# A selective scan with an FFT filter: Latin-square units, with the first group's du*B made by TensorE and ScalarE

## The chip, the cores and the metric

The kernel runs on one core of one Trainium2 chip. The metric is the device time of one execution in microseconds (us); the lower, the better. Engines are named as in the profile: PE is TensorE (PEld its weight loads), DVE is VectorE, ACT is ScalarE, POOL is GpSimd, SP is SyncE, which issues nearly all DMAs here.

## The reference, cut to what matters

The first layer is a Mamba block over 4 images of 128 channels and 128x128 pixels, taken as sequences of 16384 steps. Only the part around the scan matters for the change:

```python
u = silu(causal_conv4(x_in) + conv_b)                  # 256 channels d
dt, B, C = split(u @ x_proj_w.T, [8, 16, 16])          # 16 states s
delta = softplus(dt @ dt_proj_w.T + dt_proj_b)
A = -exp(A_log)                                        # [256, 16]
def step(h, (d, B, C, u)):
    h = h * exp(d[:, None] * A) + d[:, None] * B[None, :] * u[:, None]
    return h, einsum('ds,s->d', h, C)
y = (scan(step) + u * D) * silu(z)
out = y @ out_proj_w.T
x1 = silu(group_norm(out)) + x
```

The second layer group-normalizes x1, takes a small softmax of pooled features ("aggregation"), filters x1 through a 2D FFT with weights from that softmax, and adds half of x1. The change does not touch the second layer's FFT part.

## The kernel before, in words

`block0` computes the Mamba block and the statistics for the second layer; `block1` computes the FFT part, after it.

**Tiling.** A sequence is cut into chunks of T = 512 steps: 32 chunks per image, 128 in all. In a chunk there are 256 x 16 = 4096 independent scans. They are laid on partitions as 32 channels x 4 states (partition = 4 x channel + state), so a chunk has 32 tiles of 128 x 512: two halves of the channels (j = 0, 1), four groups of states (g = 0 to 3, the field SQ = 4 states wide), and four blocks of 32 channels (m, or ND). A **unit** is the four tiles of one (j, g); a **pair** is two tiles of it. A chunk has 8 units and NP = 16 pairs.

**Work of one pair** (`exps`, L308, and `scans`, L321 to L325): ACT computes da = exp(delta * A) from delta, repeated over the four states, into a PSUM tile of two banks; DVE runs two scans h = da * h + hb; the product of h with C goes back into hb, on DVE (L324, then h overwrites da in PSUM) or on POOL (L324, then h is in SBUF, since `dve` is false); ACT copies the last column (L325, "last") as the start of the next chunk. **Work of one unit**: POOL computes hb = du * B for all four tiles at once (`dbu`, L293); PE sums h * C over the states with a 0/1 matrix (`sums`, L337), into one PSUM bank for each half j, which `sums` opens with u * D (L334).

**Who does the products with C.** Seven of a chunk's 16 pairs go to POOL: the first pair of each unit but one; the other nine stay on DVE.

**What makes a chunk** (`pre`): load of x, three matmul stages (h1, xm, z), the convolution as 8 matmuls (L221, each two records in the trace), silu (L226, L227), the projections xd and dt, softplus (L261), du = delta * u on POOL (L269). Partitions are rearranged through DRAM: delta and du are written out and read back repeated over the four states (`rep_load`, L277), B and C are written out and read back repeated over the 32 channels (`bc_load`, L246). `post` gates y with silu(z) (L349), multiplies by the output matrix (L354), copies (L361), stores and takes statistics (L365).

**Normalization and aggregation** (`finish`): for the image before, two tiles at a time in each of 16 chunks are normalized (`norm_load`, `norm_act` L432, `norm_mm` L437, `norm_dve` L441 and L442), and two tiles in each of the next 16 chunks aggregated (`agg_load` L461, `agg_mm` L465, `agg_act` L469). For the last image there is no scan beside it.

**The order.** It is written out by hand: every piece of work has a slot and a phase, and within one slot the phases follow in a fixed order. Slots count pairs, so slot n holds the scans of pair n. Each engine runs its instructions in the order in which they are issued. The exps of a pair are issued one slot ahead, du*B two slots ahead of the unit, the sums two slots behind the unit's last pair.

```python
        for n in range(n_chunks * NP):
            todo[n - 1, "exps"].append(partial(exps, n))
            todo[n, "scans"].append(partial(scans, n))
            if n % 2 == 0:
                todo[n - 2, "dbu"].append(partial(dbu, n // 2))
            else:
                todo[n + 2, "sums"].append(partial(sums, n // 2))
        ...
                for phase in ("sums", "pe", "exps", "act", "pool", "dbu", "scans", "dve", "end"):
```

In the lists that `pre` and `post` return, slot numbers are relative to the start of the chunk before: number 16 is the first slot of the chunk itself. The text numbers slots of a chunk from 0 to 15; the preparation of the next chunk stands in the same slots (its number 2 is slot 2, its number -6 slot 10).

**PSUM.** Eight banks: two for `psum()` (all matmul stages), two for y (one for each half), four for da (two tiles of two banks).

## Time and profile before

| | |
|---|---|
| median of 8 runs | 8235.5 us (8233.16 to 8238.89) |
| the profiled execution's own time | 8235.23 us |
| its span, first to last instruction | 8233.4 us |
| block 0 with scans running | to about 7162 us |
| normalization and aggregation of the last image | 7162 to about 7358 us |
| block 1 | about 7358 us to the end |
| busy: DVE, POOL, PE, ACT | 7666.5, 7521.4, 6049.0, 5262.8 us |
| granted PE clock | 0.846 on average |

How to read the lines that follow. A group of the page reads: line, engine, operation, names (out <- in), shapes, count, then the total busy time in us, the mean of one in ns, and the idle time of the engine just ahead of these instructions with what ended it. A line of the timeline reads: start in us, length in us, engine, line, operation, names, shape, and how many consecutive instructions were merged; in brackets the wait ahead of it and what ended that. A line of the windows reads: from:to, length, busy time and count of PE, PEld, DVE, ACT and POOL, then the granted PE clock, the share of the DMA engines and GB/s.

### The profile page before, as it was taken

The page shows a single profiled execution, that of the slowest core. Times are in us where ns is not written, and L with a number is a line of the kernel's source. Part 1 is how long each engine was busy: PE and PEld are TensorE (multiplying, and loading weights), DVE is VectorE, ACT ScalarE, POOL GpSimd, SP SyncE. Part 2 cuts the span into 40 slices and gives each one's busy share as a digit, 9 for nine tenths or more (in the row PEclk, how much of TensorE's full clock was granted, in tenths as well). Part 3 has the DMA queues.
Part 4 walks back from the last instruction along what each step waited for, and adds up shares of the span by engine and source line. Part 5 has one row for each costly group of instructions (what it writes and reads, how often), then busy time and mean ns, then how long its engine had stood idle before and what let it go on. Part 6 is the DMA issues. An engine that isn't in the chain of part 4 may idle for free.

```text
span 8233.4 us, 73103 instructions
## 1 busy us (share of the span) xinstructions
PE 6049.0 (73%) x20532; PEld 2223.2 (27%) x20532; DVE 7666.5 (93%) x6640; ACT 5262.8 (64%) x9495; POOL 7521.4 (91%) x2500
## 2 busy tenths in 40 slices
PE   6776676777777777777777777777776777569999
PEld 1121121111111122221111222221111222138888
DVE  6999999999999999999999999999999999839999
ACT  5666666666666676666666666666666767534444
POOL 7999999999999999999999999999999999716665
PEclk8777778778888887888889888888998888779999
DMA  4444444444454444444454444445454444454443
GB/s 151 137 144 155 145 147 137 151 147 162 167 172 153 168 161 155 147 166 166 159 175 161 158 160 159 153 156 175 155 176 163 150 159 157 142 170 115 117 123 95
DMA packets 838679, 1257.45 MB, mean 153 GB/s; under 512 B 78200, under 2 KB 276864, under 8 KB 838272
## 3 DMA queue, kind: packets, MB, share of 16 engines
q1 hardware_dynamic: 835760, 1252.43, 46.1%
q8 instruction: 162, 2.65, 0.1%
q14 instruction: 245, 2.01, 0.1%
q10 hardware_dynamic: 2512, 0.36, 0.0%
HBM read 1009.22 MB, written 243.27 MB: 152 GB/s over the span
## 4 chain that ended last, share of the span: by engine, by line
DVE 35%; issue 25%; POOL 20%; ACT 14%; DMA 2%; PE 2%; SPq 1%; DVEq 0%; POOLq 0%; ACTq 0%
DVE da L321 14%; POOL hb L293 11%; DVE h L321 8%; POOL hb L324 7%; ACT da L308 5%; DVE hb L324 3%; DVE wb L590 3%; POOL du L269 2%; ACT L308 2%; ACT L226 2%; ACT u L226 2%; ACT zs L227 1%; DVE im L617 1%; DVE ii L620 1%; DVE ot L644 1%
## 5 line engine op out<-in xcount | busy, mean ns | idle before, releaser
L293 POOL TENSOR_TENSOR hb<-rdu,rB 128x2048 f32<-128x2048 f32 x1024 | 4631.8, 4523 | 17.9 <-DMA rdu<-dd 17.9
L321 DVE TENSOR_TENSOR_SCAN da<-da,st,hb 128x512 f32<-128x512 f32 x2232 | 2862.5, 1282 | 42.0 <-ACT da L308 2.5
L308 ACT ACTIVATE da<-rdelta,amat 128x512 f32<-128x512 f32 x4096 | 2831.9, 691 | 102.8 <-ACT st L325 0.2
L337 PE MATMUL y<-hb,sel 128*32 128x512 f32 x8192 | 1660.5, 741 | 1314.7 <-POOL hb L324 1147.1
L321 DVE TENSOR_TENSOR_SCAN h<-da,st,hb 128x512 f32<-128x512 f32 x1736 | 2127.8, 1267 | 221.5 <-ACT st L325 109.7
L324 POOL TENSOR_TENSOR hb<-h,rC 128x1024 f32<-128x1024 f32 x896 | 2103.3, 2347 | 102.9 <-DVE h L321 100.6
L324 DVE TENSOR_TENSOR hb<-da,rC 128x1024 f32<-128x1024 f32 x1152 | 1410.3, 1224 | 51.9
L325 ACT COPY st<-da 128x2 f32<-128x2 f32 x1152 | 184.4, 160 | 1929.6 <-DVE hb L324 1928.9
L221 PE MATMUL pp_cv<-xm,wck 128*128 128x512 f32 x2048 | 975.1, 631 | 57.0 <-ACT zs L215 57.0
L337 PEld LDWEIGHTS y<-hb,sel 128*32 128x32 f32 x8192 | 218.8, 116 | 2550.9 <-POOL hb L324 1780.3
L221 PEld LDWEIGHTS pp_cv<-xm,wck 128*128 128x128 f32 x2048 | 402.4, 202 | 658.3 <-issue 450.4
L616 POOL TENSOR_TENSOR re<-sq 128x520 f32<-128x520 f32 x64 | 84.8, 1325 | 464.4 <-ACT sq L614 464.3
L186 PE MATMUL pp_h<-xt,w 128*128 128x512 f32 x512 | 349.8, 807 | 199.1 <-DVE of L441 80.7
L354 PE MATMUL pp_o<-yg,wo 128*128 128x512 f32 x512 | 379.1, 881 | 126.1 <-ACT u L226 126.0
L210 PE MATMUL pp_z<-xm,win 128*128 128x512 f32 x512 | 359.8, 840 | 72.6 <-ACT xm L204 72.6
L269 POOL TENSOR_TENSOR du<-delta,u 128x512 f32<-128x512 f32 x256 | 319.3, 1267 | 60.8 <-ACT delta L261 60.8
L253 PE MATMUL pp_dt<-xd,wdt 8*128 8x512 f32 x512 | 300.4, 712 | 77.6 <-ACT xd L238 77.6
L196 PE MATMUL pp_xm<-h,w 128*128 128x512 f32 x512 | 296.3, 707 | 60.0 <-ACT h L191 60.0
L308 ACT ACT_TABLE_LOAD x261 | 334.9, 1283 | 3.0
L325 ACT COPY st<-h 128x2 f32<-128x2 f32 x896 | 171.6, 192 | 247.1 <-DVE h L321 236.4
L437 PE MATMUL pp_xr<-xr,ident 128*128 128x512 f32 x256 | 206.0, 948 | 160.3 <-DMA xr<-in_x 69.1
L590 DVE SCALAR_TENSOR_TENSOR wb<-ft,wts,wb 128x1040 f32<-128x1040 f32 x192 | 296.8, 1547 | 4.4
(107 smaller groups left out, 7372.8 us busy)
## 6 DMA issues: line engine op xcount, KB each, us to landing
rdelta<-dd SPq DMA_DIRECT2D x1024, 256.0 KB, 3.5
rdu<-dd SPq DMA_DIRECT2D x1024, 256.0 KB, 4.7
rB<-bc SPq DMA_DIRECT2D x512, 256.0 KB, 3.7
rC<-bc SPq DMA_DIRECT2D x512, 256.0 KB, 5.1
dd<-delta SPq DMA_DIRECT2D x256, 256.0 KB, 5.0
dd<-du SPq DMA_DIRECT2D x256, 256.0 KB, 3.3
ft<-in_filt_w SPq DMA_DIRECT2D x64, 520.0 KB, 7.1
xt<-in_x SPq DMA_DIRECT2D x128, 256.0 KB, 5.2
```

Source lines behind the costliest of these rows:

```text
L186: nc.tensor.matmul(ps["h", j], s.w1[:, j * P : (j + 1) * P], d["xt"], start=True, stop=True)
L210: nc.tensor.matmul(ps["z", j], w, d["xm"][:, HALO:], start=True, stop=True)
L221: nc.tensor.matmul(ps["cv", j], w, d["xm"][:, t : t + T], start=t == 0, stop=t == KC - 1)
L269: nc.gpsimd.tensor_tensor(du, d["dn"][:, j, :], d["u"][:, j, :], ALU.mult)
L293: nc.gpsimd.tensor_tensor(hb, d["du", j], d["B"][:, g : g + 1, :].to_broadcast([P, ND, T]), ALU.mult)
L308: nc.scalar.activation(da[:, q, :], d["delta", j][:, m + q, :], AF.Exp, scale=s.amat[:, c : c + 1])
L321: nc.vector.tensor_tensor_scan(h[:, q, :], da[:, q, :], hb[:, m + q, :], init, ALU.mult, ALU.add)
L324: eng.tensor_tensor(hb[:, m : m + 2, :], h, cr, ALU.mult)
L325: nc.scalar.copy(last, h[:, :, T - 1])
L337: nc.tensor.matmul(y[q * DG : (q + 1) * DG, :], s.sel, d["hb", j, g][:, q, :], start=False, stop=g == NG - 1)
L354: nc.tensor.matmul(d["po"], s.wo[:, j, :], d["yg"][:, j, :], start=j == 0, stop=j == NH - 1)
L590: nc.vector.scalar_tensor_tensor(wb, ft[:, f], s.wts[b][0:H, f : f + 1], wb, ALU.mult, ALU.add)
```

## The change

**Latin square.** A unit is no longer one group of states with four channel blocks. Unit r of a half takes position p = 0 to 3, where position p is always group p, and its channel block is `place(r, p) = (p - r) % 4`. So each unit holds one tile of every group, the four units of a half cover all (group, block) pairs, and position 0 of every unit is a tile of group 0.

**du*B of group 0** is not computed on POOL any more. In the preparation of the chunk, PE transposes du and the projections xd (time goes onto partitions), ACT multiplies the transposed du by B of each of the four states, a number per partition there, and writes the results interleaved, so that channel and state stand in the order of the scan tiles (`bt`). For every unit, PE transposes four 128x128 pieces of `bt` into a PSUM bank `b0` (`dbu_turn`), which the first scan of the unit reads directly. `dbu` on POOL covers positions 1 to 3; where `place` wraps round it needs two instructions. B of group 0 is not read back from DRAM any more.

**Pairs.** The first pair of every unit has its product with C on POOL (8 a chunk); in odd chunks one second pair too (j = 1, r = 2). DVE keeps 8, or 7 in odd chunks.

**PSUM.** y has one bank for both halves; one bank is for the transposes of the preparation, one for `b0`. The da tile of odd slots has one buffer of two banks; for even slots da is split into two tiles, the first in SBUF (two buffers), the second in PSUM (one).

**SBUF.** h1 and delta share one tag, delta has a name of its own beside the repeated delta, du stays in a buffer of its own (as before) and is now read by PE too. The gates write in place into zs. xt has one buffer (two before); the normalization's tiles have two (xr) and share three with o (four each before). The convolution's taps are loaded into a pool that is closed again, on SP.

**Order.** There are two new phases, "turn" at the head and "gate" ahead of "scans". "gate" holds the normalization's adds (`norm_dve`), which stood behind the scans; the gates of y stay in "dve", behind the scans. Both du products are issued in slot 7.

The diff, cut to its core:

```diff
-        psd = pool("psd", 2, space=PSUM)
+        pst = pool("pst", 1, space=PSUM)
+        psd = pool("psd", 1, space=PSUM)
...
-                xt = d["xt"] = p2.tile([P, T], F32, tag="xt", name=f"xt_{k}")
+                xt = d["xt"] = p1.tile([P, T], F32, tag="xt", name=f"xt_{k}")
...
-                d["h1"] = p1.tile([P, NH, T], F32, tag="h1", name=f"h1_{k}")
+                d["h1"] = p1.tile([P, NH, T], F32, tag="hd", name=f"h1_{k}")
...
-                    t = d[tag] = p2.tile([P, NG, T], F32, tag=f"r{tag}", name=f"r{tag}_{k}")
-                    for g in range(NG):
+                    t = d[tag] = p2.tile([P, NG - 1 + q, T], F32, tag=f"r{tag}", name=f"r{tag}_{k}")
+                    for g in range(1 - q, NG):
...
+            def xd_turn():
+                ps["xt"] = turned(f"xdt_{k}")
+                for t in range(NT):
+                    nc.tensor.transpose(ps["xt"][:, t, 0:NX], d["xd"][:, t * P : (t + 1) * P], s.ident[0:NX, 0:NX])
+
+            def xd_turn_act():
+                d["xdt"] = p1.tile([P, NT, NX], F32, tag="xdt", name=f"xdt_{k}")
+                nc.scalar.copy(d["xdt"], ps["xt"][:, :, 0:NX])
+
+            def du_turn(h):
+                ps["dut"] = turned(f"dut_{k}_{h}")
+                for t in range(2):
+                    for j in range(NH):
+                        at = (2 * h + t) * P
+                        nc.tensor.transpose(
+                            ps["dut"][:, 2 * t + j, :], d["du"][:, j, at : at + P], s.ident
+                        )
+
+            def bt_act(h, n0, n1):
+                if h == n0 == 0:
+                    d["bt"] = p2.tile([P, NT, NH * ND, DG, SQ], F32, tag="bt", name=f"bt_{k}")
+                for n in range(n0, n1):
+                    t, q = divmod(n, SQ)
+                    src = ps["dut"][:, 2 * t : 2 * t + 2, :].rearrange("p j (g d) -> p (j g) d", d=DG)
+                    nc.scalar.activation(
+                        d["bt"][:, 2 * h + t, :, :, q], src, AF.Copy, scale=d["xdt"][:, 2 * h + t, R + q : R + q + 1]
+                    )
...
-                (2, "act", silu_act), (3, "pe", xd_mm), (4, "act", xd_act), (5, "pe", dt_mm), (5, "act", bc_load),
-                (6, "act", dt_act), (7, "pool", partial(du_pool, 0)), (8, "pool", partial(du_pool, 1)),
-                (9, "act", partial(rep_load, 0)), (16, "pe", partial(rep_load, 1)),
+                (2, "act", silu_act), (3, "pe", xd_mm), (4, "act", xd_act), (5, "pe", dt_mm), (5, "pe", xd_turn),
+                (5, "act", bc_load), (6, "act", dt_act), (7, "act", xd_turn_act), (7, "pool", partial(du_pool, 0)),
+                (7, "pool", partial(du_pool, 1)), (9, "pe", partial(du_turn, 0)), (9, "act", partial(rep_load, 0)),
+                (10, "act", partial(bt_act, 0, 0, 3)), (11, "act", partial(bt_act, 0, 3, 8)),
+                (12, "turn", partial(du_turn, 1)), (12, "act", partial(bt_act, 1, 0, 2)),
+                (13, "act", partial(bt_act, 1, 2, 6)), (14, "act", partial(bt_act, 1, 6, 8)),
+                (16, "pe", partial(rep_load, 1)),
...
+        def place(r, p):
+            return (p - r) % ND
...
-            hb = d["hb", j, g] = p4.tile([P, ND, T], F32, tag="hb", name=f"hb_{k}_{j}_{g}")
-            nc.gpsimd.tensor_tensor(hb, d["du", j], d["B"][:, g : g + 1, :].to_broadcast([P, ND, T]), ALU.mult)
+            hb = d["hb", j, r] = hpool.tile([P, ND, T], F32, tag="hb", name=f"hb_{k}_{j}_{r}")
+            p = 1
+            while p < NG:
+                m = place(r, p)
+                n = min(NG - p, ND - m)
+                nc.gpsimd.tensor_tensor(
+                    hb[:, p : p + n, :], d["du", j][:, m : m + n, :], d["B"][:, p - 1 : p - 1 + n, :], ALU.mult
+                )
+                p += n
...
+        def dbu_turn(n):
+            k, j, r, p = pair(n)
+            d = st[k]
+            if p == 0:
+                b = d["b0"] = psd.tile([P, T], F32, tag="b0", name=f"b0_{k}_{j}_{r}")
+                for t in range(NT):
+                    src = d["bt"][:, t, j * ND + place(r, 0), :, :].rearrange("p d s -> p (d s)")
+                    nc.tensor.transpose(b[:, t * P : (t + 1) * P], src, s.ident)
...
-            da = d["da", j, g, m] = psd.tile([P, 2, T], F32, tag="da", name=f"da_{k}_{j}_{g}_{m}")
+            if p:
+                da = psd.tile([P, 2, T], F32, tag="da", name=f"da_{k}_{j}_{r}_{p}")
+                d["da", p] = [da[:, 0, :], da[:, 1, :]]
+                d["h", j, r] = da
+            else:
+                d["da", p] = [
+                    p2.tile([P, T], F32, tag="da", name=f"da0_{k}_{j}_{r}"),
+                    psd.tile([P, T], F32, tag="da1", name=f"da1_{k}_{j}_{r}"),
+                ]
...
-            dve = m > 0 or (j == 0 and g == NG - 1)
+            dve = p > 0 and not (k % 2 and j == 1 and r == 2)
...
+                b = hb[:, q, :] if p + q else d.pop("b0")
...
-                y = d["y", j] = psy.tile([P, T], F32, tag=f"y{j}", name=f"y_{k}_{j}")
+                y = d["y", j] = psy.tile([P, T], F32, tag="y", name=f"y_{k}_{j}")
...
-                nc.vector.tensor_mul(d["yg"][:, j, :], d["zs"][:, j, :], d["y", j])
+                nc.vector.tensor_mul(d["zs"][:, j, :], d["zs"][:, j, :], d["y", j])
...
-                xr = g["x", i] = p4.tile([P, T], F32, tag="xr", name=f"xr_{b}_{i}")
-                o = g["o", i] = p4.tile([P, T], F32, tag="of", name=f"of_{b}_{i}")
+                xr = g["x", i] = p2.tile([P, T], F32, tag="xr", name=f"xr_{b}_{i}")
+                o = g["o", i] = p2.tile([P, T], F32, tag="o", name=f"of_{b}_{i}", bufs=3)
...
-                x1 = g["x1", i] = p4.tile([P, T], F32, tag="xr", name=f"x1_{b}_{i}")
+                x1 = g["x1", i] = p2.tile([P, T], F32, tag="xr", name=f"x1_{b}_{i}")
...
-                    (c + 7, "pe", partial(norm_mm, i)), (c + 8, "dve", partial(norm_dve, i)),
+                    (c + 7, "pe", partial(norm_mm, i)), (c + 8, "gate", partial(norm_dve, i)),
...
+            todo[n - 1, "turn"].append(partial(dbu_turn, n))
...
-                for phase in ("sums", "pe", "exps", "act", "pool", "dbu", "scans", "dve", "end"):
+                for phase in ("turn", "sums", "pe", "exps", "act", "pool", "dbu", "gate", "scans", "dve", "end"):
```

## The prediction

> **What bounds the kernel now.** I read the page's first part, then its costliest groups, then the windows and the timeline inside one chunk, and last the two tails of block 0.
>
> ```profile
> PE 6049.0 (73%) x20532; PEld 2223.2 (27%) x20532; DVE 7666.5 (93%) x6640; ACT 5262.8 (64%) x9495; POOL 7521.4 (91%) x2500
> L293 POOL TENSOR_TENSOR hb<-rdu,rB 128x2048 f32<-128x2048 f32 x1024 | 4631.8, 4523 | 17.9 <-DMA rdu<-dd 17.9
> L324 POOL TENSOR_TENSOR hb<-h,rC 128x1024 f32<-128x1024 f32 x896 | 2103.3, 2347 | 102.9 <-DVE h L321 100.6
> L324 DVE TENSOR_TENSOR hb<-da,rC 128x1024 f32<-128x1024 f32 x1152 | 1410.3, 1224 | 51.9
> ```
>
> Two engines are full, VectorE and GpSimd; ScalarE has a third of its time free. GpSimd's largest group is the product du*B, of which the change takes a quarter away. Which of the two ends a chunk differs by stage:
>
> ```profile
> 2300.00:2357.20 57.20, 41.92 (x116) 11.56 (x112) 54.31 (x49) 37.70 (x68) 54.60 (x18) 0.85 0.49 167
> 3000.00:3054.50 54.50, 36.81 (x111) 9.96 (x109) 52.05 (x45) 37.72 (x70) 54.50 (x18) 0.82 0.46 156
> L227 ACT ACTIVATE zs<-zs x128: 1046/1055/1059, 31.4 to 7065.7; 128x1024 f32<-128x1024 f32 x128
> ```
>
> The columns are span, then PE, weight loads, DVE, ACT, POOL, clock, DMA. L227 runs once a chunk, so its starts mark the period. In a plain chunk (3000) it is 54.5 us and POOL is busy for all of it; in a chunk with normalization (2300) it is 57.2 and POOL has gaps. From 31.4 to 7065.7 are 127 periods, 7034.3 us; with periods of 54.5 and 57.2 that is about 85 of the first and 42 of the second.
>
> Inside a chunk, what one instruction really takes is the distance to the next start:
>
> ```profile
> 2299.26 2.45 DVE L321 TENSOR_TENSOR_SCAN h<-da,st,hb 128x512 f32<-128x512 f32 x2
> 2301.63 2.59 DVE L321 TENSOR_TENSOR_SCAN da<-da,st,hb 128x512 f32<-128x512 f32 x2
> 2304.25 1.22 DVE L324 TENSOR_TENSOR hb<-da,rC 128x1024 f32<-128x1024 f32 x1
> 2305.39 2.45 DVE L321 TENSOR_TENSOR_SCAN h<-da,st,hb 128x512 f32<-128x512 f32 x2
> ...
> 2327.27 2.46 DVE L321 TENSOR_TENSOR_SCAN h<-da,st,hb 128x512 f32<-128x512 f32 x2 [2.15 <-ACT st L325]
> ```
>
> ```profile
> 2297.44 4.53 POOL L293 TENSOR_TENSOR hb<-rdu,rB 128x2048 f32<-128x2048 f32 x1
> 2301.92 2.37 POOL L324 TENSOR_TENSOR hb<-h,rC 128x1024 f32<-128x1024 f32 x1
> 2304.23 4.54 POOL L293 TENSOR_TENSOR hb<-rdu,rB 128x2048 f32<-128x2048 f32 x1
> ```
>
> A pair whose product with C is on POOL costs DVE 2.37 us (2299.26 to 2301.63), a pair that stays on DVE 3.76 (2301.63 to 2305.39). On POOL, du*B costs 4.48, a product with C 2.31, and the two du products together 2.45 (2337.22 to 2339.67). POOL before: 8 x 4.48 + 7 x 2.31 + 2.45 = 54.5, the plain period exactly. DVE before: 9 x 3.76 + 7 x 2.37 = 50.4, plus bn_stats 0.59 and two gates at 0.59: 52.2. The last line shows the wait that makes the 57.2: the table loads, silu and norm work on ACT push the next exps behind DVE.
>
> **The change, part by part** (per chunk; odd and even chunks averaged).
>
> POOL. du*B covers three of four positions, in 12 instructions instead of 8: per half two of 1536 elements, two of 512 and two of 1024. From 4.48 for 2048 and 2.31 for 1024, an element costs 2.12 ns and an instruction 0.14 us, so 1536 cost 3.40 and 512 cost 1.23: 2 x 3.40 + 2 x (1.23 + 2.31) = 13.9 a half, 27.7 a chunk instead of 35.8. B is now read in full rather than repeated; I take no price for it, since the product with du of two full operands has the same rate (2.45 for two of 512). Products with C: 8 in even chunks, 9 in odd ones, 8.5 x 2.31 = 19.6 instead of 16.2. With du 2.45 the sum is 49.8 (54.5 before).
>
> DVE. 7.5 pairs at 3.76 and 8.5 at 2.37 give 48.4; with 1.8 for bn_stats and gates 50.1 (52.2 before). The scans of even slots keep one operand in PSUM and one in SBUF, as all scans have now, so I leave their price; h scans that read PSUM and SBUF take 1267 ns, da scans 1282, and either end moves the sum by under 0.2 us.
>
> So the floor of a plain chunk falls from 54.5 to 50.1. Three things are late next.
>
> ACT gains 16 bt copies of 256 elements and one xdt copy. A copy of 260 from PSUM takes 376 ns (L602); an operand per partition costs 0.1 us (512 elements: 684 in L261 against 578 in L361); two in a row overlap by 0.1 (the delta pair is 1.27 long, not 1.37). So 0.38 us each, 6.1 us, and 0.3 for xdt: 37.7 of the window becomes 44. Bounds: 0.28 each without the operand's price; 0.59 if each element, written with a gap of three words, costs twice its 0.83 ns. No row has such a write; I take 0.38, from the nearest rows. It is not hidden by the total alone, since they all stand in slots 10 to 14 beside h, xm and z. Queued behind them on ACT are the exps of the next slot, which DVE waits for. Following ACT from one "last" copy to the next (0.2, exps 1.42, then the slot's work) against DVE's 2.37 and 3.76: slots 10 and 11 hold 1.2 + 1.1 and 1.9 us, which a gate and a product of DVE nearly cover; DVE then waits some 0.5 us at slot 13 and again at slot 15. At the softplus (slot 8) it waits 0.5, at the silu (slot 4) 0.1, since the split tiles let the first scan start after one exp (0.7 earlier than in the 2.15 wait above). I take 1.6 in all; with 0.28 each it is 0.6.
>
> PE gains 44 transposes of 128 columns. Block 1's matmuls of that shape are two records of 0.14 at full clock (the stretch 7600 to 8233 holds 4468 in 615.0 us of PE), 0.28 each; at half clock about 0.43 (two records 0.215 apart at 7364). A unit's four cost 1.1 to 1.7 us, a chunk's 44 12 to 19; 0.5 a unit if a transpose is one record. PE is busy 36.8 to 41.9 us of a chunk, ends included, so it has room, but it is in order. The tight place is the transpose for slot 2: in slot 1 it stands behind all of the convolution.
>
> ```profile
> 3040.07 7.13 PE L221 MATMUL pp_cv<-xm,wck 128*128 128x512 f32 x16
> ```
>
> Convolution can start only after slot 14's bt copies, the transpose for slot 0 and a sums group, about 2.5 us into slot 15; 7.1 later comes the transpose, 1.1 more, so b0 is ready some 10.7 us after slot 15 began, and DVE wants it after 3.76 + 2.37 + 3.76 = 9.9. I charge 0.7. All other transposes have 2 to 5 us to spare, by the same walk.
>
> SP loses one B load of four. It waits already for its sources, so this is worth nothing. xt with one buffer, h1 and delta in one tag, zs gated in place and y in one bank: each old reader is done at least one slot before the new writer, except y, where the first sums of a half wait for the gate one slot earlier; PE has slack there. Nothing, or 0.3 a chunk if the slack is gone.
>
> Plain chunk: 50.1 + 1.6 + 0.7 = 52.4, 2.1 less. Chunk with normalization: the two adds and bn_stats cost DVE 2.62 (2343.35 to 2345.97), the norm activations lengthen the silu's wait by about 1.5, and the DVE work ahead of slot 8 covers 0.6 there: 52.4 + 2.62 + 0.9 = 55.9, 1.3 less. Together 85 x 2.1 + 42 x 1.3 = 233 us gained.
>
> Tails. After the last scan there is no cover:
>
> ```profile
> 7162.00:7315.00 153.00, 72.07 (x90) 20.46 (x86) 57.67 (x83) 37.76 (x58) 0.00 (x0) 0.62 0.64 204
> 7315.00:7358.00 43.00, 36.10 (x72) 12.99 (x72) 0.84 (x5) 28.35 (x73) 0.00 (x0) 0.88 0.64 200
> ```
>
> The 32 aggregation tiles run at ACT's pace, 1.07 each (7337.28 to 7338.42 and on), because four buffers hide the loads. With two, a load waits for the matmul two tiles earlier: 2.9 us from issue to landing, 0.9 of matmul, 0.4 of issue make 4.2 for two tiles, 16 x 4.2 = 67 instead of 34: 30 lost. The normalization groups (8.1 us a pair) are already held by their own stores in SP's order; three shared buffers add a wait of about 1.5 in every third group: 8 lost. The start (cwb behind the other loads on SP) and block 1 I leave, within 5.
>
> Sum: 8235.2 (the profiled execution; its span is 8233.4) - 233 + 38 = **8040**. The median of the runs, 8235.5, is the same.
>
> **The Trainium skill against this.** Two of its pages speak against terms above; the sum does not use them. "SBUF — State Buffer", Specifications, says that a 16-byte line needs two hits for full bandwidth and that each new line pays a penalty; bt is written with one word in each such line, so by it the second rival would hold. No row here shows such a write. "TensorE: Matmul & The Clock Gate", Part 4, says that transposes do not count as busy for the clock; by it the 44 transposes would run at the half-clock end of my bounds, the third rival's side. The granted clock here is 0.82 to 0.88.
>
> **Rivals.**
>
> 1. Nothing is late: ACT's and PE's waits fall into each other and the plain chunk nears 50.6, the other 54.5: 85 x 3.9 + 42 x 2.7 = 445 gained, 38 lost: 7830. For: the bt copies at 0.28. Against: ACT's waits exist already today (2.15 us). Chance 0.10.
>
> 2. **Slower: the strided bt write.** At 0.59 us each, ACT gains 16 x 0.21 = 3.4 us a chunk, in slots where it is already the last; nearly all of it (0.9) goes to DVE: 127 x 3.0 = 385 later than forecast, 8425. It decides from a copy of about 0.48 on, where 127 x 16 x 0.9 x 0.1 eats the gain of 195. Against: ACT's per-element price is the same in all its rows, 0.83. Chance 0.13.
>
> 3. PE is late: convolution at 8.7 instead of 7.1 (half clock for part of it) and transposes at 0.43: b0 comes 1.6 + 0.6 later in each chunk, less 0.5 that the silu's wait then absorbs: 127 x 1.7 = 215, so 8255. Chance 0.15, half of it faster than before.
>
> 4. POOL's pieces do not pay what I take: if a piece of 512 or 1024 costs 0.3 more beside DVE, POOL is at 52.2 and odd chunks at 53.4, and it bounds: about 8130. Chance 0.07.
>
> **Numbers.** The forecast has 0.55, within 7940 to 8130. Range 7870 to 8310: it leaves out rival 2 and the far end of rival 1, about 0.18. About 0.2% (16 us) is what a measurement can tell from no change. Faster: 0.55 + 0.10 + 0.07 + 0.06 = 0.78; same 0.05; slower 0.17.
>
> **What would show it.** The L227 period at 52.4 and 55.9; POOL's du*B groups summing to 27.7 a chunk and POOL with gaps; the bt copies near 0.47 long, 0.38 apart; DVE waits named on ACT exps around slots 13 and 15, and on a PE transpose once a chunk; the aggregation tail near 70 us. I am wrong if the bt copy is over 0.55 long, if PE is busy over 50 us of a chunk with DVE waiting for b0 more than once, or if the scans of even slots cost more than 1.3.

## The result and the profile after

The changed kernel takes 8210.3 us (median of 11 runs, 8204.9 to 8215.1) against 8236.3 before (31 runs): a ratio of 0.9969, 95% interval 0.9961 to 0.9977. It is faster, as forecast, but by 26 us and not by 195. The profiled execution has a span of 8210.9 us (8233.4 before) and a granted clock of 0.893 (0.846).

The page of the kernel after, its engines and the groups that answer to those of before:

```profile
PE 6314.3 (77%) x26164; PEld 2754.1 (34%) x26164; DVE 7420.6 (90%) x6448; ACT 6163.7 (75%) x11671; POOL 6967.2 (85%) x3204
...
L341 POOL TENSOR_TENSOR hb<-rdu,rB 128x1536 f32<-128x1536 f32 (+2 forms) x1536 | 3606.8, 2364 | 15.4 <-DMA rdu<-dd 15.4
L396 POOL TENSOR_TENSOR hb<-h,rC 128x1024 f32<-128x1024 f32 x1088 | 2571.4, 2363 | 624.8 <-DVE h L394 611.8
...
L293 ACT ACTIVATE bt<-pt_dut,xdt 128x256 f32<-128x256 f32 x2048 | 1130.8, 712 | 4.3 <-PE pt_dut L282 4.3
```

du*B on GpSimd fell from 4631.8 to 3606.8 us (28.2 a chunk, forecast 27.7), and GpSimd now idles 624.8 us ahead of its products with C, waiting for scans: it no longer bounds. Yet VectorE, the next in line, is busy for 90% only. The copies to `bt` are 0.71 us long, not 0.47.

Four plain chunks in a row and one with normalization, cut at the starts of L231 (the silu of z, L227 before); the columns are those of the prediction's windows:

```profile
3026.72:3079.16 52.44, 41.21 (x156) 14.90 (x154) 49.10 (x42) 44.57 (x87) 48.63 (x22) 0.90 0.48 157
3079.16:3133.29 54.13, 41.77 (x156) 15.50 (x156) 49.22 (x43) 44.80 (x87) 51.31 (x23) 0.91 0.47 152
3133.29:3187.39 54.10, 42.30 (x155) 15.25 (x156) 49.95 (x44) 44.81 (x87) 49.04 (x22) 0.87 0.44 152
3187.39:3241.95 54.56, 39.60 (x161) 14.46 (x160) 51.80 (x46) 44.68 (x87) 51.69 (x24) 0.97 0.46 151
2300.05:2356.25 56.20, 43.43 (x156) 16.05 (x156) 51.90 (x48) 44.76 (x86) 51.43 (x23) 0.88 0.48 165
...
L231 ACT ACTIVATE zs<-zs x128: 1047/1055/1057, 33.7 to 7014.0; 128x1024 f32<-128x1024 f32 x128
```

The plain chunk is 53.8 us on average (215.23 / 4), and the short length comes back every four chunks: 52.4, 54.1, 54.1, 54.6, then 52.45 again. The forecast was 52.4, which one in four reaches. The L231 starts span 6980.3 us instead of 7034.3, so 54 us were gained with the scans running and not 233; outside them 31 were lost again. In that gain 85 x (54.5 - 53.8) is 60, so the chunks with normalization brought about nothing: in their middle they last 56.6 us on average (55.8 to 57.8) instead of 57.2, and where they begin and end they gave that back.

VectorE's waits from 1000 to 7000 us (total, times, longest). Before, they were 109.5 us for ScalarE and 80.2 for du*B on GpSimd; after:

```profile
DVE h L394 <- ACT da L379: 127.5, 160, 1.8
DVE h L394 <- PE b L361: 112.1, 48, 3.2
DVE da L394 <- ACT da L379: 86.4, 105, 1.4
DVE da L394 <- issue: 31.9, 54, 0.9
```

The waits for GpSimd are gone, and a new releaser has come, TensorE's transposes into `b0`. The names need care: of the 127.5 us put down to ScalarE, 70.9 stand ahead of slot 2 (added up by slot from the timeline), where it is `b0` that came last. So `b0` holds VectorE up for 183 us, and ScalarE for 143, to which come the 31.9 that the profile calls "issue", all ahead of slot 13. It is seen in one chunk's timeline, TensorE, then VectorE, then ScalarE's exponentials for slot 2 (start, length):

```profile
3066.36 1.44 PE L410 MATMUL y<-hb,sel 128*32 128x512 f32 x8
3067.73 8.41 PE L225 MATMUL pp_cv<-xm,wck 128*128 128x512 f32 x16
3075.98 0.60 PE L361 MATMUL b<-ident,bt 128*128 128x128 f32 x4
```

```profile
3068.84 1.27 DVE L394 TENSOR_TENSOR_SCAN h<-da,st,b 128x512 f32<-128x512 f32 x1
...
3071.20 2.59 DVE L394 TENSOR_TENSOR_SCAN da<-da,st,hb 128x512 f32<-128x512 f32 x2
3073.82 1.22 DVE L396 TENSOR_TENSOR hb<-da,rC 128x1024 f32<-128x1024 f32 x1
3076.72 1.28 DVE L394 TENSOR_TENSOR_SCAN h<-da,st,b 128x512 f32<-128x512 f32 x1 [1.67 <-ACT da L379]
```

```profile
3071.41 1.29 ACT L379 ACTIVATE da<-rdelta,amat 128x512 f32<-128x512 f32 x2
```

Slot 0 begins at 3068.84. The transposes for slot 2 stand in TensorE's order behind the next chunk's convolution, which here takes 8.41 us; they end at 3076.58, and the scan that reads `b0` starts 0.14 later, after a wait of 1.67. The bracket names ScalarE, but its exponentials for this slot had ended at 3072.70, 4.0 us earlier: `b0` came last.

### The profile page after: what moved, and what is told of

It reads as the page before. It is cut to its first block, busy times and chain, and to the rows that moved or that the text cites. A ratio compares the mean times of both kernels' runs of the same rounds, so it can differ in the third digit from the quotient of the medians.

```text
span 8210.9 us, 87045 instructions
## 1 busy us (share of the span) xinstructions
PE 6314.3 (77%) x26164; PEld 2754.1 (34%) x26164; DVE 7420.6 (90%) x6448; ACT 6163.7 (75%) x11671; POOL 6967.2 (85%) x3204
## 4 chain that ended last, share of the span: by engine, by line
ACT 37%; DVE 31%; PE 15%; issue 9%; DMA 5%; POOL 2%; SPq 1%; DVEq 0%; ACTq 0%; POOLq 0%
ACT da L379 15%; ACT bt L293 13%; DVE da L394 10%; DVE h L394 6%; PE pp_cv L225 6%; DVE hb L396 4%; DVE wb L662 3%; PE y L410 2%; DMA dd<-delta 2%; ACT h L195 2%; DVE im L689 1%; ACT L379 1%; DVE ii L692 1%; ACT L264 1%; DMA rdelta<-dd 1%
## 5 line engine op out<-in xcount | busy, mean ns | idle before, releaser
L341 POOL TENSOR_TENSOR hb<-rdu,rB 128x1536 f32<-128x1536 f32 (+2 forms) x1536 | 3606.8, 2364 | 15.4 <-DMA rdu<-dd 15.4
L396 POOL TENSOR_TENSOR hb<-h,rC 128x1024 f32<-128x1024 f32 x1088 | 2571.4, 2363 | 624.8 <-DVE h L394 611.8
L394 DVE TENSOR_TENSOR_SCAN da<-da,st,hb 128x512 f32<-128x512 f32 x1856 | 2382.2, 1283 | 176.5 <-ACT da L379 97.2
L361 PE MATMUL b<-ident,bt 128*128 128x128 f32 x4096 | 756.6, 306 | 1010.6 <-DVE h L394 698.7
L394 DVE TENSOR_TENSOR_SCAN h<-da,st,b 128x512 f32<-128x512 f32 x992 | 1261.7, 1272 | 235.3 <-PE b L361 132.6
L394 DVE TENSOR_TENSOR_SCAN h<-da,st,hb 128x512 f32<-128x512 f32 x1120 | 1404.0, 1258 | 40.5 <-ACT da L379 40.5
L410 PE MATMUL y<-hb,sel 128*32 128x512 f32 x8192 | 1356.4, 739 | 3.0 <-POOL hb L396 3.0
L396 DVE TENSOR_TENSOR hb<-da,rC 128x1024 f32<-128x1024 f32 x960 | 1175.3, 1224 | 32.7
L293 ACT ACTIVATE bt<-pt_dut,xdt 128x256 f32<-128x256 f32 x2048 | 1130.8, 712 | 4.3 <-PE pt_dut L282 4.3
L361 PEld LDWEIGHTS b<-ident,bt 128*128 128x128 f32 x4096 | 495.1, 151 | 1671.5 <-DVE h L394 970.0
L406 PE MATMUL y<-u,diag 128*128 128x512 f32 x512 | 334.5, 739 | 338.7 <-DVE zs L420 338.7
L190 PE MATMUL pp_h<-xt,w 128*128 128x512 f32 x512 | 282.8, 680 | 47.2 <-DMA xt<-in_x 42.5
```

Of the source, the lines that this page charges most:

```text
L190: nc.tensor.matmul(ps["h", j], s.w1[:, j * P : (j + 1) * P], d["xt"], start=True, stop=True)
L293: nc.scalar.activation(d["bt"][:, 2 * h + t, :, :, q], src, AF.Copy, scale=d["xdt"][:, 2 * h + t, R + q : R + q + 1])
L341: nc.gpsimd.tensor_tensor(hb[:, p : p + n, :], d["du", j][:, m : m + n, :], d["B"][:, p - 1 : p - 1 + n, :], ALU.mult)
L361: nc.tensor.transpose(b[:, t * P : (t + 1) * P], src, s.ident)
L394: nc.vector.tensor_tensor_scan(h[:, q, :], das[q], b, init, ALU.mult, ALU.add)
L396: eng.tensor_tensor(hb, h, d["C"][:, p : p + 2, :], ALU.mult)
```

## Experiments

All ratios are against the kernel before, on the same chip (medians of 8235 to 8238 there), with 95% intervals. Three theories were on the table: **A**, TensorE's order makes `b0` late for slot 2; **B**, the strided write of the copies makes ScalarE late; **C**, transposes leave the granted clock low and so make the convolution slow.

**e1_conv_behind_turn**: the second half of the convolution one slot later, behind the transposes for slot 2.

```diff
-(0, "pe", partial(cv_mm, 1)),
+(1, "pe", partial(cv_mm, 1)),
```

> The second half of the convolution is issued one slot later, behind the transposes for slot 2. Theory A (PE's order: b0 for slot 2 stands behind the whole convolution, and VectorE waits for it, 1.6 us in a plain chunk): the distance from slot 1 to slot 2 falls from 3.9 to 6.5 us to 3.8 in every chunk, the period no longer alternates over four chunks, plain chunks go from 53.8 to about 52.3, normalization chunks gain less because the silu's wait at slot 4 comes back, and the time is about 8070 (8030 to 8110). Theory B (ScalarE is what is late, the wait for b0 only covers its wait for the silu): the wait moves to slot 4, plain chunks stay above 53.2, the time is 8160 or more.

Measured: 8098.6 us, 0.9832 (0.9817 to 0.9846). Plain chunks last 52.1 to 52.8 us, a few up to 53.4, and the beat of four is gone. VectorE's waits in the same window:

```profile
DVE h L394 <- ACT da L379: 134.5, 165, 2.3
DVE da L394 <- ACT da L379: 89.9, 105, 1.4
```

No wait on TensorE's `b0` is left, under either name. That ScalarE's totals are nearly those of before the edit is chance: their 70.9 us ahead of slot 2 are gone, and 87 stand ahead of slot 4 instead (6.5 before the edit), mostly in chunks with normalization, where ScalarE's silu and normalization work now comes last. Ahead of slots 13 and 15 next to nothing has changed. Theory A is shown: this order alone cost 112 us, with what came back at slot 4 taken off.

**e8_before_conv**: the same edit in the kernel before.

> The kernel before, with the one edit of e1_conv_behind_turn: the second half of the convolution one slot later. Theory A (the convolution's place costs time only because the change put a new wait of the scan for TensorE behind it, the b0 of slot 2): before the change no scan waits for TensorE and the plain chunk is bound by GpSimd at 54.5 us, so the time stays at 8236 within 20 us; the norm chunks may lose up to 0.5 us each, since there the silu waits for the convolution. Rival (the new place is better by itself, whatever the change): about the 112 us that it brought behind the change, 8125.

Measured: 8236.8 us, 1.0001 (0.9991 to 1.0010). The place of the convolution was free as long as no scan waited for TensorE; the change made it cost.

**e4_matmul_for_transpose**: the transposes of du and `bt` as products with the identity.

```diff
-nc.tensor.transpose(b[:, t * P : (t + 1) * P], src, s.ident)
+nc.tensor.matmul(b[:, t * P : (t + 1) * P], src, s.ident, start=True, stop=True)
```

> The 40 transposes of du and bt in a chunk are plain matmuls with the identity (two records each instead of one). Theory C (transposes do not count as busy for the clock, so the convolution after them runs partly at half clock): the granted clock rises from 0.89 to 0.95 or more, the convolution takes 7.1 us in nearly every chunk instead of one in four, the wait at slot 2 falls below 1 us, and the time to about 8150. Theory A without C: the clock stays at 0.89 to 0.91, the transposes for a unit take 0.5 us more, the wait at slot 2 grows by that: 8240 to 8280.

Measured: 8323.5 us, 1.0106 (1.0091 to 1.0121). Each is now two records instead of one; the clock rises to 0.911 from 0.893, the convolution stays at a mean of 8.27 us, and the wait grows (after: 112.1 us in 48 times):

```profile
DVE h L394 <- PE b L361: 214.2, 78, 3.9
```

Theory C is not borne out: the products go with a granted clock that is a little higher over the whole, but the convolution does not get shorter, and the queue gets longer. The clock did not reach the 0.95 that the theory asked for.

**e2_state_major** and **e3_both**: partitions ordered 32 x state + channel, so that the copies write runs of 32 words; e3 has e1's edit too.

```diff
-d["bt"] = p2.tile([P, NT, NH * ND, DG, SQ], F32, tag="bt", name=f"bt_{k}")
+d["bt"] = p2.tile([P, NT, NH * ND, SQ, DG], F32, tag="bt", name=f"bt_{k}")
...
-return ap.rearrange("d (o t) -> d o t", o=1).to_broadcast([DG, SQ, T])
+return ap.partition_broadcast(SQ)
```

> Partitions are state-major (32 x state + channel) in all scan tiles, so bt is written in runs of 32 words instead of one word in four; results and instruction counts are the same. Theory B (the gap in the written words doubles ScalarE's price for an element and that makes ScalarE late): bt copies fall from 0.71 us and 0.47 apart to 0.47 and 0.38, the waits ahead of slots 13 and 15 fall from 0.65 and 0.84 to about 0.2 together, convolution starts a little earlier, time about 8040 (8000 to 8080). Theory A (PE's order is the larger part): the waits at 13 and 15 fall, the one at slot 2 stays at 1.4 or more, time about 8110. If the price is that of the operand per partition or of reading PSUM: bt copies unchanged, 8210.

> Both edits together. If A and B are separate waits, their gains add: about 7930 (7880 to 7980), and plain chunks come near 51.3, the sum of VectorE's work being 50.1. If one wait covers the other, the gain is no more than that of the better of the two, 8040 to 8070.

Measured: 10140.6 us, 1.2314 (1.2295 to 1.2332), and 10103.0 us, 1.2267 (1.2246 to 1.2287). The copies did get shorter, 471 ns in e2, but the loads broke: GpSimd waits 1425 us for those of du, 15 in the kernel after. SyncE's queue, the load of the repeated du (ns: least, median, most), in the kernel after and in e2:

```profile
L309 SPq DMA_DIRECT2D rdu<-dd x1024: 512/602/2622, 49.1 to 7056.8; - x171
```

```profile
L312 SPq DMA_DIRECT2D rdu<-dd x1024: 712/2480/5412, 60.7 to 8985.8; - x171
```

A load of du is written here as 4 times 32 rows, with the repeat outside; in the kernel after it is 32 rows of 4 copies each. The repeat outside is not what makes it slow: the loads of C have it outside in the kernel after (32 times 4 rows) and four of them take 2.5 us on SyncE's queue, and inside in e2 (4 rows of 32 copies), where four take 8.3. What the slow forms share is the outer count of 4, and the quick ones here and below have 16 or 32; no run sets that alone. Nor is each issue slow: the delta loads just ahead, of the same form, have a median of 537 ns, so the time builds up behind the first few.

Two things were changed at once, and the second swamped the first. The next runs keep the loads as they are.

**e6_contiguous_bt, e14_runs_of_2, e15_runs_of_4**: e1 with nothing but `bt`'s order changed, to runs of 32, 2 and 4 words (the edit of e6 is shown). The scans then read group 0's du*B with channels and states exchanged, through the same instructions.

```diff
-d["bt"] = p2.tile([P, NT, NH * ND, DG, SQ], F32, tag="bt", name=f"bt_{k}")
+d["bt"] = p2.tile([P, NT, NH * ND, SQ, DG], F32, tag="bt", name=f"bt_{k}")
...
-d["bt"][:, 2 * h + t, :, :, q], src, AF.Copy
+d["bt"][:, 2 * h + t, :, q, :], src, AF.Copy
```

> The kernel of e1_conv_behind_turn (8098.6 us), with the scaled copies of the transposes written in runs of 32 words instead of every fourth word; the loads from DRAM keep their order. The states and channels of group 0's du*B then stand on other partitions than the rest expects, so group 0's part of the output has its channels and states exchanged; every instruction of the rest is as before. Theory B (the strided write is what makes ScalarE late for the scans of slots 13 and 15): the copies start 0.36 us apart instead of 0.48, as in e2_state_major, which takes 16 x 0.12 = 1.95 us a chunk off ScalarE; the waits ahead of slots 13 and 15 (0.65, and 0.27 or 1.4 by turns) fall to about a third, some 1.0 us a chunk, and the time to 7970. Rival B1 (not the stride but the number of copies in the slots 10 and 12, which are short, sets these waits): under half of it goes, 8050. Rival B2 (the vector engine waits for something else there, such as the last-column copies): 8095.

> e1_conv_behind_turn (8098.6 us, copies of 712 ns that start 0.48 us apart) with the scaled copies written in runs of 2 words, 32 bytes apart. Like e6_contiguous_bt (runs of 32 words: 480 ns, 0.36 apart, 7916 us) it exchanges channels and states of group 0, and the rest is as before. Two theories of what the stride costs. Lines: a write pays for each 16 bytes of the buffer that it touches; one word a line makes 256 of them and 32-word runs 64, so 2-word runs touch 128, a third of the way: about 0.56 us long and 0.40 apart. Breaks: each break in the run costs, 256 of them against 8, so with 128 about half the way: 0.60 long and 0.42 apart. Time between 7916 and 8098 in the same proportion: 7975 or 8005.

> The same with runs of 4 words (16 bytes, 64 bytes apart). Lines: 64 lines, as with 32-word runs, so the copy takes 0.48 us, 0.36 apart, and the time is that of e6_contiguous_bt, 7916. Breaks: 64 of them, about a quarter of the price left: 0.54 long, 0.385 apart, 7960. This is the run that tells the two apart; a copy near 0.71 would mean that both are wrong and only a long run is written fast.

Measured: 7916.4 us, 0.9612 (0.9597 to 0.9626); 7919.7 us, 0.9618 (0.9602 to 0.9634); 7918.1 us, 0.9613 (0.9598 to 0.9627). The copies of e1 and of e14:

```profile
L293 ACT ACTIVATE bt<-pt_dut,xdt 128x256 f32<-128x256 f32 x2048 | 1133.6, 714 | 9.7 <-PE pt_dut L282 9.7
```

```profile
L293 ACT ACTIVATE bt<-pt_dut,xdt 128x256 f32<-128x256 f32 x2048 | 831.1, 498 | 21.0 <-PE pt_dut L282 21.0
```

Starts are 0.48 and 0.36 us apart (e15 and e6: 480 ns, 0.36). Theory B is shown, and it is the larger of the two: 180 us. Neither law in the expectations for the price holds: runs of 2 words should have kept a third or half of it and kept under a tenth. In e6 a plain chunk is 51.0 or 51.4 us by turns (50.7 or 51.4 in the first image), the waits ahead of slots 13 and 15 (0.65 us, and 0.27 or 1.4) are gone but for some 0.9 us in odd chunks ahead of 14 and 15, part of it for GpSimd, and those named for ScalarE have halved (from 1000 to 6700 us, where e1 has 131.6 and 86.3; 71 of the 87.0 stand ahead of slot 4):

```profile
DVE h L394 <- ACT da L379: 87.0, 95, 1.8
...
DVE da L394 <- ACT da L379: 12.8, 44, 1.0
```

**e9_other_slot_to_pool** and **e10_copies_earlier**: the other way to treat those waits, by moving work away from them (e1's strided write stays).

```diff
-dve = p > 0 and not (k % 2 and j == 1 and r == 2)
+dve = p > 0 and not (k % 2 and j == 1 and r == 0)
```

```diff
-(9, "pe", partial(du_turn, 0)),
-(10, "act", partial(bt_act, 0, 0, 3)), (11, "act", partial(bt_act, 0, 3, 8)),
+(8, "pe", partial(du_turn, 0)),
+(9, "act", partial(bt_act, 0, 0, 4)), (10, "act", partial(bt_act, 0, 4, 5)), (11, "act", partial(bt_act, 0, 5, 8)),
```

> e1_conv_behind_turn, with the one product per odd chunk that GpSimd takes over from VectorE moved from slot 13 to slot 9. Theory: in slot 13 ScalarE has four of the scaled copies and needs about 3.5 us, so that the 1.4 us that VectorE saves there come back as a wait ahead of slot 15 (1.4 us in odd chunks, 0.27 in even ones); slot 9 has no copies, so the saving stays: odd chunks 1.1 us shorter, 64 of them 70 us, 8030. Rival (ScalarE is late by its sum over slots 9 to 15, not by one slot): the wait moves to slot 11 or 13, 8090. Below 8000 would mean that slot 13's short length also held up the chunk after it.

> e9_other_slot_to_pool, with the first transposes of du one slot earlier and their eight scaled copies in slots 9 to 11 as 4, 1 and 3 instead of in 10 and 11 as 3 and 5. Theory: the wait of 0.65 us ahead of slot 13 is there because ScalarE has 8 copies (3.8 us) in slots 10 and 11 beside its exponentials, while slot 9 has none and lasts 3.8 us; with 4 in slot 9 that wait goes, 127 x 0.6 = 76 us below e9_other_slot_to_pool, about 7955. Rival (slot 9, shortened in odd chunks by the product moved there, now waits instead): even chunks gain and odd ones lose the same, so near e9's time; then the product and the copies belong in different slots.

Measured: 8068.3 us, 0.9797 (0.9781 to 0.9814), and 8015.6 us, 0.9731 (0.9717 to 0.9746). e9 brought 30 of the 70 us expected. In plain odd chunks a new wait of 1.8 us for GpSimd stands ahead of slot 10 (in the waits: DVE's h for L396 on POOL, 51.2 us in 30 times) and takes the saving back: with slot 9's product on GpSimd too, slots 8, 9 and 10 in a row each need one of the two buffers of h. So the wait moved, as the rival said, though to another place and for another reason than it named. e10 brought 53 of 76: the wait ahead of slot 13 is gone in plain chunks, while the 1.8 us ahead of slot 10 stay in odd ones and 0.5 (even) to 0.8 us (odd) on average ahead of slot 15. Moving the work about brought less (83 us from e1) than making the copies shorter (182).

**e12_state_major_split_loads**: e3 with each load cut into one transfer per state.

```diff
-nc.sync.dma_start(out=t[:, g, :], in_=replicated(d["dd"][q, r : r + DG, :]))
+for n in range(SQ):
+    nc.sync.dma_start(out=t[n * DG : (n + 1) * DG, g, :], in_=d["dd"][q, r : r + DG, :])
```

> The whole computation with the partitions ordered 32 x state + channel (as in e2_state_major, so that the scaled copies write runs of 32 words), the convolution placed as in e1_conv_behind_turn, and each of the repeated loads cut into one transfer per state (32 partitions, 64 KB), so that no transfer has the repeat outermost. Theory: e2_state_major was slow only through the form of its loads (an issue of 2480 ns on SyncE's queue, where the form before takes 602); with the loads cut, the gain of e6_contiguous_bt is to be had in full: 7916, if SyncE issues four times as many loads (92 a chunk) within the chunk of 51 us, that is at under 0.5 us each. Rival B3 (the issue costs about 0.6 us whatever its size): 92 x 0.6 = 55 us a chunk, SyncE sets the period, 8300 to 8500. Rival B4 (DRAM rows read again at a distance are slow in themselves): the transfers stay late and the time near 10000.

Measured: 8360.3 us, 1.0150 (1.0134 to 1.0165).

```profile
L312 SPq DMA_DIRECT2D rdu<-dd x4096: 302/419/1792, 59.7 to 7210.9; - x196
```

The transfers are quick again (1.9 us to landing, 4.4 in the kernel after), so it was the form of e2's loads and not the order in which DRAM is read: rival B4 falls. But 92 issues of 0.42 us fill 39 us of SyncE's chunk, and what is queued behind them comes late: TensorE waits 463 us for the input tile xt, 29 in the kernel after. This is the size of B3, by another sum.

**e13_agg_buffers**: e10 with four buffers for the last image's aggregation.

```diff
-x1 = g["x1", i] = p2.tile([P, T], F32, tag="xr", name=f"x1_{b}_{i}")
+tag, bufs = ("o", 3) if b == B - 1 and i // 2 % 2 else ("xr", 2)
+x1 = g["x1", i] = p2.tile([P, T], F32, tag=tag, name=f"x1_{b}_{i}", bufs=bufs)
```

> e10_copies_earlier (8015.6 us), with the loads of the last image's aggregation spread over four buffers (two of the tag xr, two of the tag o by turns) instead of two. Theory of the prediction's tail term (two buffers make a load wait for the matmul two tiles earlier, 30 us): from the last scan to the first matmul of the stage behind it the time falls from 235.7 us to about 206, and the whole to 7986. Rival (the tail is longer since the loads stand behind the last image's stores on SyncE's queue): no change, 8015.

Measured: 7985.6 us, 0.9695 (0.9679 to 0.9711). The aggregation behind the last scan, in the kernel after and in e13 (windows):

```profile
7256.00:7336.00 80.00, 44.56 (x72) 12.95 (x72) 7.64 (x13) 30.45 (x77) 0.00 (x0) 0.80 0.51 141
```

```profile
7056.00:7108.00 52.00, 35.23 (x72) 12.09 (x72) 8.12 (x13) 30.44 (x77) 0.00 (x0) 0.88 0.75 218
```

With the same work the stretch falls from 80 to 52 us, and its DMA share rises from 0.51 to 0.75. From the last normalized tile to the last aggregated one it is 71.2 us in the kernel after, 42.5 in e13 and 43.0 before the change; the rest of the stretch lies ahead of block 1. e13 differs from e10 in the buffers alone and is 30 us faster, as expected: two buffers were the cause.

**e16_pairs_in_order**: the computation whole, partitions ordered 8 x channel pair + 2 x state + channel of the pair, each load cut in two, with e1's and e13's edits.

```diff
-nc.sync.dma_start(out=t[:, g, :], in_=replicated(d["dd"][q, r : r + DG, :]))
+for e in range(2):
+    nc.sync.dma_start(out=t[e::2, g, :], in_=replicated(d["dd"][q, r + e : r + DG : 2, :]))
```

> The whole computation with nothing exchanged: partitions ordered 8 x channel pair + 2 x state + channel of the pair, so that the scaled copies write runs of 2 words as in e14_runs_of_2 and every tile agrees; each repeated load is cut into two transfers of 64 partitions (every second one), the convolution stands as in e1_conv_behind_turn and the last aggregation has four buffers as in e13_agg_buffers. Theory: the price of the stride is the copies' alone, and two issues of 0.45 to 0.6 us on SyncE for each load (46 a chunk, 21 to 28 us) stay hidden in a chunk of 51 us, as 92 of 0.42 us in e12_state_major_split_loads did not: 7920 less the 31 us of the buffers, 7890. Rival (the loads take the gain back also at twice the number, through SyncE's order): 8000 to 8200.

Measured: 7900.4 us, 0.9596 (0.9580 to 0.9612), 310 us below the changed kernel and the fastest of all. From its page:

```profile
PE 6301.7 (80%) x26164; PEld 2760.7 (35%) x26164; DVE 7403.7 (94%) x6448; ACT 5900.5 (75%) x11671; POOL 6950.2 (88%) x3204
...
L294 ACT ACTIVATE bt<-pt_dut,xdt 128x256 f32<-128x256 f32 x2048 | 830.3, 496 | 6.7 <-PE pt_dut L283 6.5
```

The copies have e14's price, VectorE is at 94%, and twice as many load issues (0.59 us each) are left with the 10 us by which it misses 7890, if the other gains add up. So the 180 us were no effect of the exchanged channels and states.

## Why the prediction was wrong, point by point

- **GpSimd and the floor: right.** du*B takes 28.2 us a chunk for 27.7, so rival 4 falls, GpSimd is idle in every chunk shown, and with most waits gone the plain chunk comes to 50.7 to 51.4 (e6), of which 50.1 was forecast as VectorE's work.
- **PE, "I charge 0.7": too small, and by the wrong part.** Ahead of slot 2 the four chunks lose 0.2, 1.75, 1.9 and 2.6 us, 1.6 on average (taken from start to start, as the waits below are: idle time and the 0.08 us by which two instructions in a row overlap). The walk itself was right: the convolution starts 2.76 us into slot 15, in the chunk shown and on average (forecast 2.5), and the wait is for the b0 of slot 2. The transposes are even cheaper than forecast, 0.6 us for four, near the 0.5 that it named for one record each. What failed is the 7.1 us, taken from one row. That row, the first line here, ran at a granted clock of 1.00; below it stand the four convolutions of the windows shown above (time, busy time of PE and of its weight loads, granted clock, DMA):

```profile
3040.07:3047.20 7.13, 7.13 (x16) 2.94 (x16) 1.00 0.77 259
```

```profile
3067.73:3076.14 8.41, 8.41 (x16) 3.44 (x16) 0.84 0.58 195
3121.56:3130.37 8.81, 8.80 (x16) 3.59 (x16) 0.81 0.60 203
3176.60:3185.19 8.59, 8.59 (x16) 3.57 (x16) 0.83 0.50 170
3230.23:3237.36 7.13, 7.13 (x16) 2.94 (x16) 1.00 0.76 253
```

  The length times the clock granted during it is 7.1 in each line, and in all 128 chunks of both kernels (7.10 to 7.14): the clock accounts for the whole difference. In the slow ones the first matmul records start 0.85 us apart and the rest 0.43.

  The convolution near the end of one window sets the length of the next: 8.41 is followed by 54.13, 8.80 by 54.10, 8.59, which starts late, 3.4 us into slot 15, by 54.56, and 7.14 by 52.45. Over all 128 chunks it takes 7.14 us in a fifth of the cases and 8.27 on average. The trace of before held the warning: 7.14 in 62%, up to 10.08, mean 7.62. This is rival 3, half clock for part of the convolution, with cheap transposes, in three of four chunks. That its 8255 is the nearest number on the page is in part luck: it put 1.7 us a chunk on top of the forecast, and 0.9 came.
- **The bt copies, "I take 0.38, from the nearest rows": the costliest step.** They start 0.48 us apart and last 0.71, over the 0.55 that was named as a sign of being wrong. That nearest row wrote every word; these write one in four. The bound of 0.59 was too high and 0.38 too low, and 0.48 is just where rival 2 was said to eat the gain: its law gives 8040 + 183 = 8223. So each of rivals 2 and 3 alone would nearly give the measured time, and it took e1 and e6 to show that both were at work. Runs of 2 words bring 0.36 and 180 us. The Trainium skill's "SBUF — State Buffer", Specifications, states that a 16-byte line needs two hits for full bandwidth, and that is what the runs show: one word a line costs 714 ns, two words 498, four 480. Its other clause, a price for every new line, is at most the 18 ns between the last two.
- **ACT's waits, 1.6 forecast:** 0.65 ahead of slot 13, 0.84 (0.27 and 1.41 by turns) ahead of 15, 0.38 ahead of 8, together 1.9. The places were right, but that the size nearly was is luck. With the copies 0.36 apart (e6), close to the 0.38 that the walk assumed, 0.9 is left: the walk charged too much for its copies, and the longer ones filled the charge. With 50.1 and the 1.6 of TensorE the 1.9 make 53.6, for 53.8 measured.
- **The Trainium skill's rule on the clock** ("TensorE: Matmul & The Clock Gate", Part 4): by it, transposes would not count as busy. They were added here and the granted clock rose from 0.846 to 0.893; as products (e4) it is 0.911. The convolution's mean is 8.27 us either way, so the lower clock in the convolution is not shown to come from the transposes.
- **Chunks with normalization, 1.3 gained each:** about 0.2 on average, over the 51 periods in which something of it runs. In their middle they gained 0.6, and where they end nothing (the last one of each image is 61.5 to 61.9 long, 59.2 before). TensorE's order is a small part of it: in e1 VectorE's wait for ScalarE at slot 4 (1.4 to 2.3 us) is there in place of the wait at slot 2, and they still last 56.3 in their middle. The strided write is the larger part: in e6 they last 54.1 or 55.1, under the forecast 55.9.
- **Tails, 38 lost: right in sum.** From the last scan to block 1 it took 231.5 us instead of 198.3: 33 lost, 28 of them between the last normalization and the last aggregation tile (30 forecast, and e13 gives all of it back). The 8 for normalization did not come (it gained 3); 8 came between the last aggregation and block 1, whose first input load is issued 3.0 us after the last aggregated tile, where it was issued 0.8 us ahead of it before. Why it comes later was not tested.
- **The sum.** Of the 233 us that the chunks should have gained, 179 are missing: 85 x (53.8 - 52.4) = 119 in the plain chunks, the rest in those with normalization. The two mis-sized steps, undone, are worth 112 (e1) and 182 (e6) and lead to 7916 together. That is 294 us, more than the 170 by which the forecast missed, since 127 x 0.7 = 89 of it was already charged for slot 2 and the waits for ScalarE were charged too high. The forecast without its charge for slot 2 would be 8040 - 89 = 7951. So with the two causes taken away the other terms of the sum hold within 35 us together, errors both ways included, and the mechanism of e6 is nearly that of rival 1 (plain chunk 50.6, measured 50.7 to 51.4).

## What to carry to other kernels

When work moves to an engine with room, look for the first thing that it makes another engine wait for, and put that ahead of the long jobs in the engine's order: here one place in TensorE's list was worth 112 us, while the same edit before the change was worth nothing. Take the duration of what stands in such a queue from all its occurrences, not from one row, and on TensorE read the clock that was granted during each. And price a write by its stride: an element per gap is not an element in a run, and an order with pairs of words can be enough.

## What the runs showed of the hardware

- ScalarE's scaled copy of 256 fp32 elements from PSUM takes 712 ns if every fourth word is written, 498 in runs of 2 words, 480 in runs of 4 or 32.
- A transpose of 128x128 in fp32 is one record, and four take 0.60 us; the product with the identity is two.
- A load that fills 128 partitions from 32 rows of DRAM (du) or from 4 (C) issues in 602 ns in the median on SyncE's queue when it is written as 32 times 4. Written as 4 times 32 such loads back up (2480 ns for those of du, behind others of that form), whether the repeat is the outer or the inner count, and the kernel lost 23%. Cut into transfers of 32 partitions an issue is 419 ns, of 64 partitions 592.
- The same 16 matmuls of the convolution last 7.14 to 9.2 us, and their length times the clock granted during them is 7.1 us in every chunk. Plain chunks show a period of four, where nothing in the program has one. What lowers the clock there, and why with that period, no run shows, since none set the clock by itself.
